# Issue order of two attention looks: where the look for maxima is narrow and the look for weights wide, the wide one goes first

## The chip, the cores and the metric

The kernel runs on one core of one Trainium2 chip. The metric is the time of one execution on the device in microseconds (us), smaller being better; the median of several runs is compared. A profile of one execution shows when each instruction ran on each engine: TensorE (PE; its weight loads are listed apart as PEld), VectorE (DVE), ScalarE (ACT), GpSimd (POOL) and SyncE (SP), which issues most of the DMA transfers.

## What is computed

Two network layers over 16 sequences of 512 tokens with 128 features each. In each layer the input is normalized, two branches are computed from it, and both are added to it.

```
xn = layernorm(x);  x = x + memory_attention(xn) + conv_attention_mixture(xn)     # first layer
xn = layernorm(x);  x = x + causal_conv_attention(xn) + routed_experts(xn)        # second layer
```

The first layer's second branch has a convolution, an attention with 16 heads of 8 features without a mask, and 8 dense experts. Its first branch is a recurrent memory update over chunks of 64 tokens. The second layer's first branch attends twice, causally, with a convolution between:

```
def _causal_attn(q, k, v):
    scores = jnp.einsum('bthd,bshd->bhts', q, k) * scale
    scores = jnp.where(mask, scores, -jnp.inf)
    attn = jax.nn.softmax(scores, axis=-1)
    return jnp.einsum('bhts,bshd->bthd', attn, v)
ctx = _causal_attn(q, k, v);  q2 = conv(ctx);  out = _causal_attn(q2, k, v) @ out_w.T
```

Its second branch routes each token to 8 of 32 small experts.

## The kernel before

Everything is written as stages: Python generators that issue some instructions and then yield. The class `Turns` (line 276) runs them in turns. In a turn each live stage is stepped once, in the order of its priority (0 first). TensorE's instructions stay in the order in which they are issued (line 690: a manual schedule for TensorE); the order on the other engines is chosen by a scheduler in the framework, which also gives out the buffers. Where a priority-1 or later stage issues VectorE instructions, they are held behind the last maxima reduction of the same turn (`newest`, `tc.issue_after`, lines 293 to 295); from priority 2 on GpSimd's also stand behind the last mask (`cleared`, lines 297 and 298).

Attention is done for one sequence, one pass and one half of the heads at a time, in two stages.

- `largest` (priority 0, line 378) finds the maximum of the scores of each query. One **look for maxima** takes one block of 128 queries for one or more heads in two row groups: matmuls into two PSUM banks (`s1`, in the trace `s<-kx,qx`), then on VectorE a reduction into `nm`. Without a mask, and with a mask where one head fills the bank, it is one instruction a bank (line 403 or 395); otherwise an addition of the mask (line 402) and a reduction (line 403).
- `weighted` (priority 1, line 427) makes the softmax weights. One **look for weights** recomputes scores the other way round into two banks (`s2`, in the trace `s<-qx,kx`), ScalarE takes exponentials into `e` (line 475), and in the second layer GpSimd clears the triangle above the diagonal (line 483), or VectorE does late in the kernel, once the routing is counted (line 481). Between the matmuls and the exponentials, eight older weights may be multiplied with the values (`pc`, through `tail` and `values`).

`widths` (line 359) says how wide a look is. Without a mask there are 16 looks of 512 keys for each half of the heads. With the causal mask there are 11: four of 512, four of 384, two of 256 (two heads at once) and one of 128 (four heads at once). So a bank is always filled to 384 or 512 elements, but a 256 or 128 look needs the addition and the reduction. There are 64 such sets in the second layer. A lock (`p1`, `p2`) lets one set of each kind run at a time, so a turn holds at most one look for maxima and one for weights, normally of different sets.

After a set's last look for maxima, `largest` splits the maxima into `mp` (lines 409 and 410), transposes them on TensorE (`tpm`, line 417), copies them to `m` and sends them by DMA through memory into extra rows of `qx`; the looks for weights of that set read `qx`.

Beside the looks a turn holds units of the first layer's experts (`first` and `second` in `ffn`: matmuls `phe` and `pye`, ScalarE `hTe` and `y`), and pieces of all other stages. Scores, expert units and most other products share seven PSUM banks (`work`, line 177); the framework gives a new tile the bank that it expects to be free first, and the tile's first matmul waits until the bank's earlier contents are read. `fill` (line 199) adds idle matmuls where a turn would leave TensorE with little work. How many expert units a turn gets follows from sums over the turn (`load_ns`, `look_ns`), taken after both looks.

The lines around the change are 290 to 300 (a turn's order), 384 to 404 (a look for maxima) and 461 to 492 (a look for weights).

Of the kernel before, what the change touches and what calls it, by code (L numbers as in the profile page):

```python
# [17 lines left out]
P = 128  # L18
# [64 lines left out]
def network(ctx: ExitStack, tc: tile.TileContext, a, out):  # L83
# [55 lines left out]

    pools, done, locks, clock, newest, cleared, held, read, cell = {}, {}, set(), [0], [None], [None], [0], [0], []  # L140

    lent = set()

    def mark(*m):
        done[m] = clock[0]
# [17 lines left out]
    def room():  # L163

        while held[0] >= pools["work"]:
            yield
# [109 lines left out]
    class Turns:  # L276
# [6 lines left out]
        def run(self, until=None):  # L283
            while (self.stages or self.live) and (until is None or not until()):
                self.live += [x[1:] for x in self.stages if x[0] <= self.turn]
                self.stages = [x for x in self.stages if x[0] > self.turn]
                self.live.sort(key=lambda x: x[0])


                newest[0] = cleared[0] = None  # L290
                step = lambda x: next(x[1], StopIteration) is not StopIteration
                left = [x for x in self.live if x[0] == 0 and step(x)]
                with ExitStack() as behind:
                    if newest[0] is not None:
                        behind.enter_context(tc.issue_after(newest[0].ins))
                    left += [x for x in self.live if x[0] == 1 and step(x)]
                    if cleared[0] is not None:
                        behind.enter_context(tc.issue_after(cleared[0].ins))
                    left += [x for x in self.live if x[0] > 1 and step(x)]
                self.live = left  # L300
                self.turn += 1
                fill()
                held[0] -= read[0]
                read[0] = 0
                mean_ns[0] += (other_ns[0] - mean_ns[0]) / 32
                load_ns[0] = look_ns[0] = 0.0
                locks.discard("values")
                clock[0] = self.turn
# [50 lines left out]
    def widths(causal):  # L359

        for i in range(TB):
            n = S if not causal else S - i * P
            per = {S: 1, 3 * P: 1, 2 * P: 2, P: 4}[n]
            for t in range(0, NH, per):
                yield i, n, per, t
# [12 lines left out]
    def largest(slot, causal):  # L378


        q, k, at = slot
        yield from acquire("p1")
        nm = att.tile([P, TB, 2, NH], F32, tag="nm", bufs=2, name="nm")
        for i, n, per, t in widths(causal):
            qt = TB - 1 - i

            look_ns[0] = {S: 2050, 3 * P: 1800, 2 * P: 2450, P: 3000}[n] if causal else 1750
            sv = [work("s1")[:, 0 : per * n].rearrange("p (i n) -> p i n", i=per) for r in range(2)]
            for u in range(per):
                for r in range(2):  # L390
                    rr = slice(64 * r, 64 * r + 64)
                    mm(sv[r][:, u, :], q[rr, t + u, qt * P : (qt + 1) * P], k[rr, t + u, :n])
            for r in range(2):
                if causal and per == 1:
                    newest[0] = nc.vector.tensor_tensor_reduce(  # L395
                        out=sv[r][:, 0, :], in0=sv[r][:, 0, :], in1=row["caus"][:, S - n :], scale=1.0, scalar=-BIG,
                        op0=ALU.add, op1=ALU.max, accum_out=nm[:, qt, r, t : t + 1],
                    )
                    continue
                if causal:  # L400
                    dg = sv[r][:, :, n - P : n]
                    nc.vector.tensor_tensor(dg, dg, bc(row["caus"][:, S - P :], 1, per), ALU.add)  # L402
                newest[0] = nc.vector.tensor_reduce(nm[:, qt, r, t : t + per], sv[r], AX.X, ALU.max)  # L403
            yield
        locks.remove("p1")
        padded = maxima.pop(0)
        maxima.append(padded)
        mp = padded[:, 0 : TB * 16].rearrange("p (t r i x) -> p t r i x", t=TB, r=2, i=2)
        nc.vector.tensor_scalar(mp[:, :, :, 0, :].bitcast(FR), nm, -1.0, None, ALU.mult)
        nc.vector.scalar_tensor_tensor(  # L410
            mp[:, :, :, 1, :].bitcast(FR), nm, -1.0, mp[:, :, :, 0, :], ALU.mult, ALU.subtract
        )
        yield
        yield from room()

        tp = work("tpm")
        nc.tensor.transpose(tp[:, 0:P], padded, ident)
        m = att.tile([TB * 16, P], FR, tag="m", bufs=1, name="m")
        nc.scalar.copy(m, tp[0 : TB * 16, 0:P])
        nc.sync.dma_start(at, m.bitcast(F32))  # L420
        at = at.rearrange("(a r i t) s -> r i t a s", r=2, i=2, t=NH)
        for r in range(2):
            rows = q[64 * r + 32 : 64 * r + 34, :, :].bitcast(F32)
            nc.sync.dma_start(rows.rearrange("i t (a s) -> i t a s", s=P), at[r])
        yield

    def weighted(slot, vp, c, causal, cn, name):


        q, k, _ = slot  # L430
        yield from acquire("p2")
        cnv = cn.rearrange("p t (a c j d) -> p (t a) c j d", c=2, j=2, d=DH)
        old, last = [], []
        got = []

        def values(heads):
            for head in heads:
                kt, n, t, r, e = head
                lent.discard(id(head))
                g = 2 * (t % 2) + r  # L440
                j = t // 2
                mm(
                    got[0][32 * g : 32 * g + 32, S - n :], vp[:, kt, 4 * g + 2 * c + j, :], e,
                    start=(kt == 0 and j == 0), stop=(kt == TB - 1 and j == 1),
                )
            if kt == TB - 1 and t == NH - 1:
                cs = att.tile([P, S], F32, tag="cs", bufs=1, name="cs")
                nc.scalar.copy(cs, got[0])
                locks.remove("ctx")
                last.append(cs)  # L450

        def tail(least):
            if not got and "ctx" not in locks:
                locks.add("ctx")
                got.append(pools["ps"].tile([P, 512], F32, tag="ctx", bufs=1, name="pc"))
            if got and len(old) >= least:
                locks.add("values")
                for _ in range(min(len(old) // 4, 2)):
                    values([old.pop(0) for _ in range(4)])

        for i, (kt, n, per, t) in enumerate(widths(causal)):
            while len(old) >= pools["heads"] and not got and "ctx" in locks:
                yield
            s = [work("s2")[:, 0 : per * n] for r in range(2)]
            sv = [x.rearrange("p (i n) -> p i n", i=per) for x in s]
            for u in range(per):
                for r in range(2):
                    rr = slice(64 * r, 64 * r + 64)
                    mm(sv[r][:, u, :], k[rr, t + u, kt * P : (kt + 1) * P], q[rr, t + u, S - n :])
            tail(pools["heads"])  # L470

            pool = pools["weights"][i % len(pools["weights"])]
            e = pool.tile([P, 2, 512], F32, tag="e", bufs=3, name="e")
            for r in range(2):
                nc.scalar.activation(e[:, r, 0 : per * n], s[r], AF.Exp, scale=SCALE)  # L475
            ev = e[:, :, 0 : per * n].rearrange("p r (i n) -> p r i n", i=per)
            if causal:
                for r in range(2):
                    if ("counted",) in done:
                        dg = ev[:, r, :, 0:P]  # L480
                        nc.vector.scalar_tensor_tensor(dg, bc(row["tri"], 1, per), BIG, dg, ALU.mult, ALU.min)
                        continue
                    cleared[0] = nc.gpsimd.affine_select(  # L483
                        out=ev[:, r, :, 0:P], in_=ev[:, r, :, 0:P], pattern=[[0, per], [1, P]],
                        compare_op=ALU.is_ge, fill=0.0, base=0, channel_multiplier=-1,
                    )
            for u in range(per):
                for r in range(2):
                    old.append((kt, n, t + u, r, ev[:, r, u, :]))
                    if pool is pools["mid"]:  # L490
                        lent.add(id(old[-1]))
            yield
        locks.remove("p2")
        free_slots.append(slot)
        turns.stages.append((turns.turn, 2, ends(summed(old, tail, last, c, cnv), name)))
# [1146 lines left out]
```

## Time and profile before

| what | value |
|---|---|
| runs, us | 3588.07, 3590.16, 3597.58 (median 3590.16) |
| the profiled execution, us | 3586.38 |
| its span from first to last instruction, us | 3584.7 |
| mean granted TensorE clock | 0.969 |
| look for maxima on VectorE, one bank, 512 / 384 keys (line 395), ns | 708 / 579, plus 141 to read the result |
| 256 / 128 keys: addition (line 402), ns | 427 / 694 |
| 256 / 128 keys: reduction (line 403), ns | 680 / 680 |
| exponentials of one bank (line 475), 512 / 384 elements, ns | 600 / 491 |
| TensorE busy from 1850 to 3300 us | 1419.1 of 1450 us, clock 0.99 |
| TensorE busy from 3300 us to the end | 237.6 of 284.7 us, clock 0.86 |

The durations are those from 1850 to 3300 us, in the second layer. The span is the time from the first to the last instruction; the profiled execution's own time has about 2 us more around it. A busy share says how long an engine had an instruction in work. A matmul's listed duration is longer than the distance to the next one, since matmuls are pipelined; distances from start to start tell how fast the stream runs. In a list of waits, "A <- B" means that A's engine stood idle until B's result was there. In the 40 slices of the page each digit is a tenth.

### The profile page before, as it was taken

What the parts mean: (1) busy time and instruction counts of PE and PEld (TensorE: products, weight loads), DVE (VectorE), ACT (ScalarE), POOL (GpSimd) and SP (SyncE); (2) the same over time, 40 slices, a digit from 0 to 9 for tenths busy, and PEclk for the clock granted to TensorE, in tenths of its full rate; (3) what the DMA queues carried; (4) which work ended last, traced back from release to release, by engine and by line L of the source; (5) the groups of instructions that cost most, each with busy time, mean ns of one, the idle gap of its engine ahead of it and who ended that gap; (6) DMA issues with size and microseconds to landing.
All of it is one profiled execution on the core that took longest, in us unless ns stands there. A gap on an engine that the chain in (4) does not pass through costs nothing.

```text
span 3584.7 us, 63937 instructions
## 1 busy us (share of the span) xinstructions
PE 3388.3 (95%) x22085; PEld 1903.2 (53%) x22085; DVE 2319.8 (65%) x6045; ACT 2217.0 (62%) x4919; POOL 1541.4 (43%) x2386
## 2 busy tenths in 40 slices
PE   6999999899999999999999999999999999998887
PEld 3445555454555455555555555555555555553444
DVE  5676666566756565556467676666666666667885
ACT  1566656665666787766656666666666666664444
POOL 5423532433531455433544444434444444433653
PEclk7999999899999999999999999999999999998997
DMA  5222222212222233334344444444344434433343
GB/s 176 70 70 71 74 72 78 67 53 85 76 73 88 89 110 108 110 118 125 106 111 136 126 121 113 121 136 122 95 132 121 134 114 111 132 106 98 92 102 91
DMA packets 289794, 370.37 MB, mean 103 GB/s; under 512 B 45984, under 2 KB 141376, under 8 KB 289088
## 3 DMA queue, kind: packets, MB, share of 16 engines
q1 hardware_dynamic: 282304, 359.46, 34.7%
q0 software_dynamic: 7168, 6.82, 1.2%
q8 instruction: 177, 2.90, 0.3%
q14 instruction: 145, 1.19, 0.1%
HBM read 236.58 MB, written 132.99 MB: 103 GB/s over the span
## 4 chain that ended last, share of the span: by engine, by line
PE 50%; DVE 4%; DMA 2%; ACT 2%; POOL 1%; issue 1%; SPq 1%; POOLq 0%; DVEq 0%; ACTq 0%
PE s L197 13%; PE pye L610 10%; PE phe L197 10%; PE pc L197 8%; PE pq L197 1%; DVE s L395 1%; PE fill L206 1%; PE tpc L251 1%; PE tp L251 1%; DVE nm L403 1%; PE po L197 1%; DVE s L402 1%; ACT e L475 1%; PE pjk L197 1%; PE pv L197 1%
## 5 line engine op out<-in xcount | busy, mean ns | idle before, releaser
L475 ACT ACTIVATE e<-s 128x512 f32<-128x512 f32 (+1 forms) x2432 | 1274.6, 576 | 556.6 <-PE s L197 514.3
L403 DVE TENSOR_REDUCE nm<-s 128x1 f32<-128x512 f32 (+2 forms) x1408 | 906.7, 682 | 512.0 <-PE s L197 510.6
L395 DVE CUSTOM_DVE_ANT_0 s<-s,sb_const 128x512 f32<-128x512 f32 (+1 forms) x1024 | 623.4, 643 | 388.2 <-PE s L197 386.6
L483 POOL TENSOR_SCALAR_AFFINE_SELECT e<-e 128x128 f32<-128x128 f32 (+2 forms) x1270 | 426.7, 344 | 746.6 <-ACT e L475 721.1
L197 PE MATMUL s<-kx,qx 64*128 64x512 f32 (+3 forms) x3072 | 624.4, 431 | 44.4 <-ACT e L475 15.4
L197 PE MATMUL pc<-e,vp 128*32 128x512 f32 (+3 forms) x6144 | 625.8, 506 | 13.4 <-POOL e L483 7.2
L610 PEld LDWEIGHTS pye<-ew,hTe 128*128 128x128 f32 x4096 | 519.8, 193 | 177.9 <-issue 157.6
L197 PEld LDWEIGHTS s<-kx,qx 64*128 64x128 f32 x3072 | 272.8, 187 | 574.4 <-issue 226.6
L610 PE MATMUL pye<-ew,hTe 128*128 128x128 f32 x4096 | 563.0, 281 | 1.5 <-ACT hTe L600 1.4
L197 PE MATMUL s<-qx,kx 64*128 64x512 f32 (+3 forms) x3072 | 536.3, 357 | 26.9 <-DVE nm L403 7.8
L197 PE MATMUL phe<-x1T,ew 128*128 128x512 f32 x1024 | 547.5, 619 | 7.0 <-DMA ew<-in_ew 3.0
L600 ACT ACTIVATE hTe<-phe,sb_cols 128x512 f32<-128x512 f32 x512 | 353.7, 691 | 240.7 <-PE phe L197 238.1
L197 PEld LDWEIGHTS s<-qx,kx 64*128 64x128 f32 x3072 | 305.7, 189 | 78.5 <-ACT e L475 20.4
L618 POOL TENSOR_TENSOR ac<-ac,y 128x512 f32<-128x512 f32 x128 | 163.7, 1279 | 422.6 <-ACT y L617 359.9
L402 DVE TENSOR_TENSOR s<-s,sb_const 128x256 f32<-128x256 f32 (+1 forms) x384 | 181.6, 515 | 190.0 <-PE s L197 157.1
L197 PEld LDWEIGHTS pc<-e,vp 128*32 128x32 f32 x6144 | 150.9, 110 | 238.9 <-issue 174.9
L197 PEld LDWEIGHTS phe<-x1T,ew 128*128 128x128 f32 x1024 | 157.9, 192 | 73.1 <-issue 43.5
L617 ACT ACTIVATE y<-pye,pr 128x128 f32<-128x128 f32 x512 | 146.8, 369 | 31.1 <-PE pye L610 26.9
L395 DVE DVE_READ_ACCUMULATOR2_ANT nm<- 128x1 f32 x1024 | 144.0, 141 | 0.0
L212 POOL TENSOR_SCALAR rs_t<-ss 128x4 f32<-128x4 f32 (+1 forms) x56 | 11.5, 206 | 228.6 <-ACT sq L265 227.3
L1458 POOL DMA_INDIRECT acc<-eo,sidx x32 | 51.6, 1612 | 74.3 <-DVE eo L1452 26.6
L212 POOL TENSOR_SCALAR rs_t<-ln_mv 128x4 f32<-128x4 f32 x64 | 12.7, 198 | 162.5 <-DVE ln_mv L222 159.7
(297 smaller groups left out, 3935.7 us busy)
## 6 DMA issues: line engine op xcount, KB each, us to landing
ew<-in_ew SPq DMA_DIRECT2D x256, 256.0 KB
kx<-rk SPq DMA_DIRECT2D x192, 256.0 KB
qx<-rq SPq DMA_DIRECT2D x128, 256.0 KB
rq<-hi SPq DMA_DIRECT2D x64, 256.0 KB
rq<-lo SPq DMA_DIRECT2D x64, 256.0 KB
rk<-hi SPq DMA_DIRECT2D x64, 256.0 KB
rk<-lo SPq DMA_DIRECT2D x64, 256.0 KB
qx<-r SPq DMA_DIRECT2D x64, 256.0 KB
```

The lines of the kernel that those rows point to most:

```text
L197: nc.tensor.matmul(o, lhsT=lhsT, rhs=rhs, start=start, stop=stop)
L251: nc.tensor.transpose(tp[:, t * P : (t + 1) * P], src(t), ident)
L395: newest[0] = nc.vector.tensor_tensor_reduce(out=sv[r][:, 0, :], in0=sv[r][:, 0, :], in1=row["caus"][:, S - n :], scale=1.0, scalar=-BIG, ...
L402: nc.vector.tensor_tensor(dg, dg, bc(row["caus"][:, S - P :], 1, per), ALU.add)
L403: newest[0] = nc.vector.tensor_reduce(nm[:, qt, r, t : t + per], sv[r], AX.X, ALU.max)
L475: nc.scalar.activation(e[:, r, 0 : per * n], s[r], AF.Exp, scale=SCALE)
L483: cleared[0] = nc.gpsimd.affine_select(out=ev[:, r, :, 0:P], in_=ev[:, r, :, 0:P], pattern=[[0, per], [1, P]], compare_op=ALU.is_ge, fill= ...
L600: nc.scalar.activation(hs[i], ph, AF.Relu, bias=col("fb", i))
L610: nc.tensor.matmul(pye[0][:, t, :], lhsT=h[:, t * P : (t + 1) * P], rhs=w2[e][:, f, :], start=(f == 0 and t == 0), stop=(f == 3), skip_gro ...
L617: nc.scalar.mul(y[:, t, :], pye[0][:, t, :], pr[:, t, e : e + 1])
L618: nc.gpsimd.tensor_tensor(ac, ac, y, ALU.add)
L1458: nc.gpsimd.indirect_dma_start(out=acc, out_offset=bass.IndirectOffsetOnAxis(ap=sidx[:, e : e + 1], axis=0), in_=eo[:, i, :], in_offset=No ...
```

## The change

The last look that each of the two stages has issued now leaves behind how wide its next look will be: `coming[0]` for the maxima, `coming[1]` for the weights, and 0 where the set is at its end. At the start of a turn `narrow` is true when the next look for maxima is of 256 or 128 keys and the next look for weights of 384 or 512. In such a turn the priority-1 stages are stepped before the priority-0 stages, outside the block that holds VectorE's instructions behind the last reduction; in all other turns the order is as before.

```diff
-    lent = set()
+    lent, coming = set(), [0, 0]
...
                 step = lambda x: next(x[1], StopIteration) is not StopIteration
-                left = [x for x in self.live if x[0] == 0 and step(x)]
+                left, narrow = [], 0 < coming[0] < 3 * P <= coming[1]
+                if narrow:
+                    left += [x for x in self.live if x[0] == 1 and step(x)]
+                left += [x for x in self.live if x[0] == 0 and step(x)]
                 with ExitStack() as behind:
                     if newest[0] is not None:
                         behind.enter_context(tc.issue_after(newest[0].ins))
-                    left += [x for x in self.live if x[0] == 1 and step(x)]
+                    if not narrow:
+                        left += [x for x in self.live if x[0] == 1 and step(x)]
                     if cleared[0] is not None:
                         behind.enter_context(tc.issue_after(cleared[0].ins))
...
-        for i, n, per, t in widths(causal):
+        looks = list(widths(causal))
+        for at_look, (i, n, per, t) in enumerate(looks):
...
                 newest[0] = nc.vector.tensor_reduce(nm[:, qt, r, t : t + per], sv[r], AX.X, ALU.max)
+            coming[0] = [*looks, (0, 0)][at_look + 1][1]
             yield
...
-        for i, (kt, n, per, t) in enumerate(widths(causal)):
+        looks = list(widths(causal))
+        for i, (kt, n, per, t) in enumerate(looks):
...
+            coming[1] = [*looks, (0, 0)][i + 1][1]
             yield
```

## The prediction

> **What bounds the kernel now.** I read the page first: busy shares, slices and clock.
>
> ```profile
> span 3584.7 us, 63937 instructions
> PE 3388.3 (95%) x22085; PEld 1903.2 (53%) x22085; DVE 2319.8 (65%) x6045; ACT 2217.0 (62%) x4919; POOL 1541.4 (43%) x2386
> ...
> PE   6999999899999999999999999999999999998887
> ...
> PEclk7999999899999999999999999999999999998997
> ```
>
> TensorE is busy 95% of the span, and the granted clock is 9 tenths or more almost everywhere. The reordered turns lie in the second layer, so next I asked for TensorE's waits between 1850 and 3300 us, most of that stretch.
>
> ```profile
> engine line waited for: us in total, times, longest us
> ...
> PE s L197 <- DMA qx<-top: 5.9, 7, 2.2
> PE phe L197 <- DMA ew<-in_ew: 3.0, 1, 3.0
> ...
> PE tpc L251 <- ACT cs L448: 2.1, 5, 0.5
> ...
> PE tpm L417 <- DVE mp L410: 1.0, 3, 0.4
> PE phe L197 <- ACT e L475: 0.8, 5, 0.2
> PE s L197 <- DVE nm L395: 0.7, 2, 0.3
> ```
>
> The answer's 18 rows add up to 28 us of 1450. That is about the stock from which a change that adds and removes no work could win here. Waits for VectorE's maxima and ScalarE's weights, the two things that are reordered, are about 2 us of it. (A wait counts only from the modelled end of the matmul before, so short ones look smaller than they are; below I take intervals from start to start for that.) In the last stretch, 3300 to 3584.7 us, TensorE is busy 237.6 of 284.7 us, at a clock of 0.86, and VectorE 208.4: that stretch is looser.
>
> Third, the order of time in one such pair of turns: a look for maxima of two heads by 256 keys, then one of four by 128.
>
> ```profile
> start us, us, engine line op out<-in xcount [idle before <-releaser]
> ...
> 2028.66 0.50 PE L197 MATMUL s<-kx,qx 64*128 64x256 f32 x4
> ...
> 2029.00 0.40 PE L197 MATMUL s<-qx,kx 64*128 64x512 f32 x2
> 2029.27 0.43 DVE L402 TENSOR_TENSOR s<-s,sb_const 128x256 f32<-128x256 f32 x1 [0.35 <-PE s L197]
> ...
> 2029.33 0.66 PE L251 MATMUL tpc<-sb_const,cs 128*128 128x128 f32 x4
> 2029.50 1.09 ACT L475 ACTIVATE e<-s 128x512 f32<-128x512 f32 x2 [0.61 <-PE s L197]
> ...
> 2032.09 0.66 PE L197 MATMUL s<-kx,qx 64*128 64x128 f32 x8
> ...
> 2032.59 0.45 PE L197 MATMUL s<-qx,kx 64*128 64x512 f32 x2
> 2032.86 0.70 DVE L402 TENSOR_TENSOR s<-s,sb_const 128x512 f32<-128x512 f32 x1 [0.85 <-PE s L197]
> ```
>
> Matmuls named s<-kx,qx are the look for maxima, s<-qx,kx the look for weights. From start to start the maxima's look holds TensorE for 0.34 us at 256 keys (2028.66 to 2029.00) and 0.50 at 128; the weights' look for 0.33 (2029.00 to 2029.33). VectorE starts 0.61 us after its look, ScalarE 0.50 after its own, and both had been idle.
>
> **The change, part by part.** It adds no instruction on any engine and takes none away: the built programs have the same instructions by kind and tile. On TensorE the order differs in 181 turns: 118 with a 256-key look, 63 with a 128-key look, all but six against a weights' look of 512. By the trace 164 of them lie before 3300 us, the first at 1647. In 180 nothing stands between the two looks. VectorE's order differs in under 3% of its places, ScalarE's in ten instructions, GpSimd's in eight, SyncE's DMAs in nine single issues moved by one to three places; none of the transfers changes its size, and I put these at nothing beside the terms below.
>
> *The stream of matmuls.* I took medians of the time from each pair's start to the next start in the second layer. A look's first pair after other work takes 0.337 us (512 keys, the maxima's; the weights' look hardly ever comes first and is taken as the same), 0.223 (256), 0.164 (128); a pair inside the block 0.119 or 0.117 (256) and 0.110 to 0.112 (128); the last pair, before other work, 0.325 (512), 0.209 (256) and 0.203 (128, seen only before value matmuls). For 256: before 0.223+0.119+0.325 = 0.667, after 0.337+0.117+0.209 = 0.663, no change. For 128: before 0.164+2x0.110+0.112+0.325 = 0.821, after 0.337+3x0.110+0.203 = 0.870, so 0.05 more, times 63: **+3.1 us**. Ends: 0 (leaving after 128 costs no more than staying) and +9 (0.05 in all 181).
>
> *VectorE 0.33 us later.* The maxima are read from PSUM later by the weights' look, 0.33 us. VectorE itself has room: 129.1 us of idle time before the 100 pairs of 256-key additions from 1850 to 3300, 1.3 us a look, and 31.6 us before the 50 of 128 keys, 0.6 a look. What can be late is the next matmul into the same bank. I joined the trace's times with the bank numbers of the built program: from VectorE's last read to the next matmul into the bank is 0.147 us where TensorE had waited. After a 128-key look the usual successor is the next turn's weights' look, 56 times, with 0.51 us in the median: 0.36 of slack, just over 0.33. Over the 328 banks of the reordered looks before 3300, 53 have less than 0.33 us of slack, and the shortfall adds up to 9.3 us; later 9 of 30, 2.3 us. The banks rotate differently afterwards, in the new order nearer for the 128-key look (five to seven tiles on, where it was mostly seven or eight), farther for others. Ends 0 and 11.6; I take half, **+5.8**.
>
> *The chain behind the last look.* The 128-key look ends a set of maxima; mp, the transpose tpm, m and a DMA into qx follow, and the first look for weights waits for that. TensorE waited for mp 7 times in the second layer and for qx<-top 7 times before 3300; 0.33 us on all 14 is 4.6. Ends 0 and 4.6, taken half: **+2.3**.
>
> *ScalarE 0.34 to 0.50 us earlier.* This is the gain. Before 3300, 24 of 328 banks of the weights' looks were taken over by a matmul that had waited for that read, later 8 of 34: at most 32 x 0.36 = 11.5 us. The five waits of tpc for cs, 2.1 us, stand behind the same exponentials, but where I looked ScalarE was at y or hTe and couldn't have begun earlier. Ends 0 and -13.6; I take half, **-6.8**.
>
> *The masks of the last stretch.* From 3384 us on, VectorE clears the weights' upper triangles (L481). The built order now puts these, which wait for the exponentials, ahead of or between the narrow look's additions and reductions. In the turn at 3391.85 us of the trace, additions that started at 3393.12 would start at some 3393.7, with 0.48 us of masks done before them and not after: at most 0.3 late in each of the ten reordered turns from there on, +3; values that are ready earlier may give 2 back. Between these ends I take **+1**.
>
> A rule speaks against any longer wait. The one long stall, 2.99 us for ew, was followed by a clock of 0.72 from 2494 to 2498 us, and four passes of phe took 3.31 us; two take 1.13 in the turn shown. Counting such a loss, some 1.1 us, for each of the seven waits for qx would add up to 8 us. The Trainium skill ("TensorE: Matmul & The Clock Gate", section "Why this matters for your kernels") says that gaps over about 3 us throw the clock back. By it 0.33 us added to waits of at most 2.2 adds nothing; no run here shows where the limit lies. My sum has nothing for it.
>
> Sum: 3.1+5.8+2.3-6.8+1 = **+5.4 us**, on the profiled execution's 3586.4 (span 3584.7, the rest lies around it): 3591.8. The median of the runs shown is 3590.2, so on that scale **3596 us**, 0.2% over. A measurement of this kernel tells about 0.3%, 10.8 us, from no change: the forecast is no change, with its own range 3583 to 3601.
>
> **Rivals.**
> *Late maxima hold TensorE up (slower).* If slack counts for less than I think, since a late look makes the next late too, each turn pays 0.33. The point from which this decides is 10.8/0.33 = 33 turns of 181; the slacks show 62 short banks, some two to a turn. At 50 turns, with 3.1 for the stream: 3590+16.5+3 = 3610. For: five-tile distance after 128 keys. Against: over 0.6 us of idle VectorE before each narrow look.
> *Earlier exponentials pay (faster).* All 13.6 us are won, and delays cost nothing: 3590-13.6 = 3577. For: those waits recur in the same turn of each set. Against: TensorE waits for ScalarE in few places, and the second matmul of a pair often waited for hTe, which isn't earlier.
> *The masks stall VectorE in the last stretch (slower).* If each of those ten turns waits for both exponentials, 0.6 us each by the page, it is +12, with the stream's 3.1 3605; it decides from 0.8 us a turn. For: VectorE already waits 16.0 us there for exponentials before masks. Against: it comes to the masks backlogged in the turns I read.
> That the change doesn't do what it says is ruled out by the 181 turns.
>
> **How the numbers follow.** Forecast 0.50, late maxima 0.24, masks 0.08, earlier exponentials 0.18. So faster by over 0.3% 0.18, within 0.50, slower 0.32. The range reaches from the faster rival to just past late maxima: 3577 to 3613; outside is left about 0.2.
>
> **What would show it.** Right: TensorE's busy time within some 5 us; VectorE's idle time before L402 up by about 0.33 us a look; exponentials of these turns starting 0.5 us after the turn does; the waits of TensorE from 1850 to 3300 still near 28 us. Wrong: waits s<-nm of over 10 us (late maxima); the stretch after 3300 longer by over 6 (masks); waits for e and cs gone and nothing in their place (the gain).

## The result and the profile after

The changed kernel has a median of 3608.56 us (3605.81 to 3611.12, six runs); the kernel before, on the same chip and in turn with it, 3590.18 us. The ratio is 1.0045, 95% interval [1.0032, 1.0058], some 16 us slower. A second set, `after_again` below, gave 1.0026 [1.0013, 1.0039]. So it is slower, by about the 0.3% that the prediction took this kernel's measurement to tell. The time lies inside the whole range, 3577 to 3613, but outside the forecast's own 3583 to 3601: "no change" was the wrong side of the border. The profiled execution took 3607.65 us, with a span of 3605.9 and a mean granted clock of 0.966.

The head of the page of the kernel after, with the slices of TensorE and of its granted clock:

```profile
span 3605.9 us, 63924 instructions
...
PE 3396.2 (94%) x22085; PEld 1920.4 (53%) x22085; DVE 2319.0 (64%) x6045; ACT 2214.3 (61%) x4919; POOL 1541.1 (43%) x2386
...
PE   6999999899999999999999999999999999998887
...
PEclk7999999899999999999999999999999999998988
```

The counts behind the x are those of before, and VectorE, ScalarE and GpSimd are busy as long within 3 us. TensorE's busy time rose by 8 us and the span by 21. Nothing here says where.

TensorE's waits from 1850 to 3300 us, kernel after (engine, line and tile, "<-" what it waited for; us in total, times, longest):

```profile
PE s L197 <- DMA qx<-top: 5.4, 5, 2.2
PE s L197 <- ACT hTe L608: 5.1, 21, 0.8
PE tpm L423 <- DVE mp L416: 2.5, 7, 0.5
...
PE tpc L251 <- ACT cs L454: 1.8, 4, 0.5
PE tpc L251 <- ACT e L482: 1.5, 5, 0.4
...
PE phe L197 <- ACT e L482: 0.7, 2, 0.4
PE s L197 <- DVE nm L400: 0.7, 2, 0.3
PE s L197 <- DVE nm L408: 0.7, 2, 0.4
```

The second line is new: 21 times a look's matmul waits until ScalarE has read an expert unit's bank (`hTe`). Waits for `mp` went from 1.0 to 2.5 us. The waits that the wide looks' earlier exponentials should have taken away (`e`, `cs`) are where they were, and one for `e` was added (`tpc`, 1.5). No row is large, but the sum is: the rows of this answer add up to 29.3 us, those of before to 28, and of the 28 one row has left the window. The first line is of the kernel before, from 1850 to 3300 us, the second of the kernel after, from 3300 us on:

```profile
PE pt L197 <- DVE bd L1346: 6.3, 1, 6.3
...
PE pt L197 <- DVE bd L1354: 5.9, 1, 5.9
```

Without it 22 us of waits became 29. Because a wait counts only from the modelled end of the matmul before, I measured the rest from start to start, below.

The same pair of turns as in the prediction, now from 2032.38 us (timeline of the kernel after; start, duration, what):

```profile
2032.38 0.50 PE L197 MATMUL s<-qx,kx 64*128 64x512 f32 x2
...
2032.71 0.63 PE L197 MATMUL s<-kx,qx 64*128 64x256 f32 x4
...
2032.98 0.74 DVE L338 SCALAR_TENSOR_TENSOR lo<-pjk,sb_cols,hi 128x512 fp32r<-128x512 f32 x1
...
2033.62 0.66 PE L251 MATMUL tpc<-sb_const,cs 128*128 128x128 f32 x4 [0.28 <-ACT e L482]
...
2033.97 0.75 DVE L407 TENSOR_TENSOR s<-s,sb_const 128x256 f32<-128x256 f32 x2
...
2036.05 0.50 PE L197 MATMUL s<-qx,kx 64*128 64x512 f32 x2
...
2036.16 1.14 ACT L625 ACTIVATE y<-pye,pr 128x128 f32<-128x128 f32 x4 [0.20 <-PE pye L618]
2036.39 0.56 PE L197 MATMUL s<-kx,qx 64*128 64x128 f32 x8
...
2037.06 0.70 DVE L407 TENSOR_TENSOR s<-s,sb_const 128x512 f32<-128x512 f32 x1 [1.15 <-PE s L197]
2037.17 0.61 ACT L482 ACTIVATE e<-s 128x512 f32<-128x512 f32 x1
```

And from the 128-key turn of the kernel before, which begins at 2032.09 us:

```profile
2032.20 1.14 ACT L617 ACTIVATE y<-pye,pr 128x128 f32<-128x128 f32 x4 [0.20 <-PE pye L610]
...
2033.21 1.10 ACT L475 ACTIVATE e<-s 128x512 f32<-128x512 f32 x2
```

In the 256-key turn the addition begins 1.59 us after the turn (2032.38 to 2033.97), before 0.61: VectorE had begun other work (`lo`, and before and after it `vp`). The turn takes 3.67 us, before 3.43. In the 128-key turn the exponentials begin 1.12 us after the turn's start, the very delay of before (2032.09 to 2033.21): ScalarE is at `y` in both, so scores that are ready 0.5 us earlier start nothing earlier.

To place the loss I compared each turn's length from 1640 to 3290 us, from the start of its first look to the next turn's, in both traces. The differences fall into two kinds. **Short ones**, up to 0.65 us, recur at the same place in set after set: +2.4 us in all in the second 256-key turn, +3.2 in the 128-key turn, +4.8 in the 512-key turn behind it, together **+9.9 us** with small remainders elsewhere. **Jumps** of one to two us come in single turns, of both signs, and sum up to +8 us. After 3300 us another 3 are lost. The experiments take the two kinds apart.

### The profile page after: what moved, and what is told of

Its sections match the earlier page's. It is cut to its first block, busy times and chain, and to the rows that moved or that the text cites. A ratio compares the mean times of both kernels' runs of the same rounds, so it can differ in the third digit from the quotient of the medians.

```text
span 3605.9 us, 63924 instructions
## 1 busy us (share of the span) xinstructions
PE 3396.2 (94%) x22085; PEld 1920.4 (53%) x22085; DVE 2319.0 (64%) x6045; ACT 2214.3 (61%) x4919; POOL 1541.1 (43%) x2386
## 4 chain that ended last, share of the span: by engine, by line
PE 49%; DVE 5%; DMA 3%; ACT 2%; issue 1%; POOL 1%; SPq 1%; POOLq 0%; DVEq 0%; ACTq 0%
PE s L197 12%; PE pye L618 10%; PE phe L197 10%; PE pc L197 8%; DVE s L400 1%; PE pq L197 1%; DVE nm L408 1%; PE tpc L251 1%; PE tp L251 1%; PE fill L206 1%; ACT e L482 1%; DVE s L407 1%; PE po L197 1%; PE pjk L197 1%; ACT hTe L608 1%
## 5 line engine op out<-in xcount | busy, mean ns | idle before, releaser
L197 PE MATMUL s<-kx,qx 64*128 64x512 f32 (+3 forms) x3072 | 616.5, 421 | 49.2 <-ACT e L482 16.8
L197 PEld LDWEIGHTS s<-kx,qx 64*128 64x128 f32 x3072 | 290.6, 187 | 528.9 <-issue 212.9
L197 PE MATMUL s<-qx,kx 64*128 64x512 f32 (+3 forms) x3072 | 545.3, 367 | 25.8 <-DVE nm L408 7.9
```

Of the source, the lines that this page charges most:

```text
L197: nc.tensor.matmul(o, lhsT=lhsT, rhs=rhs, start=start, stop=stop)
```

## The experiments

All were timed in five rounds against the kernel before on the same chip. "Short waits" is the sum just described, from 1640 to 3290 us, each kernel's trace against the trace of before. Line numbers shift by a few between kernels.

| run | median, us | ratio to before [95%] | short waits, us |
|---|---|---|---|
| `before_again` | 3593.28 | 0.9994 [0.9979, 1.0008] | +0.2 |
| `after_again` | 3606.43 | 1.0026 [1.0013, 1.0039] | +9.2 |
| `x128` | 3598.82 | 1.0012 [1.0000, 1.0024] | +5.8 |
| `x256` | 3602.75 | 1.0016 [1.0006, 1.0027] | +3.4 |
| `late_dve` | 3608.30 | 1.0040 [1.0025, 1.0054] | +9.5 |
| `notlate` | 3602.74 | 1.0018 [1.0006, 1.0030] | +9.2 |
| `lateonly` | 3599.05 | 1.0004 [0.9988, 1.0020] | -1.2 |
| `before_light` | 3575.64 | 0.9941 [0.9920, 0.9962] | -11.2 |
| `after_light` | 3583.54 | 0.9960 [0.9946, 0.9973] | -9.3 (by sum) |
| `reord` | 3600.78 | 1.0018 [1.0005, 1.0030] | +0.8 |

(`after_light` was compared with `before_light`, +1.9; -11.2 and +1.9 make -9.3.)

**Is the measure itself steady?** The kernel before once more:

> The kernel before unchanged, for a second trace of it. Both the late-read theory and its rivals expect 1.000 within 0.001 of itself. Its short waits from 1640 to 3290 us should agree with the first trace within 1.5 us if what I read off as short steady waits is a property of the order; its half-speed time of TensorE may differ by 10 us or more if that is a property of the run. If the short waits differ by 5 us or more, the 9 to 10 us read from the changed kernel's traces can't be told from scatter.

Its short waits agree to 0.2 us, and those of `lateonly` below, which has the order of before up to 3384 us, to 1.2: so 9 to 10 us are no scatter. Its jumps don't agree: +7.1 us against the first trace of the very same kernel, nearly the +8 of the kernel after. So jumps of this size come without the change; the clock below goes with most of them. The kernel after once more:

> The changed kernel once more, beside the others on the same chip and with a second profile. The steady part of the loss (waits for banks in the narrow turns and the turn behind a 128-key look, 10 us between 1640 and 3300 us in the first profile) should be the same to 1 us, since it is fixed by the program. The rest of the first profile's loss (half-speed windows, 8 us there) depends on where the windows of 3.4 us fall and may move. Ratio 1.003 to 1.005.

The short waits come back, 9.2 against 9.9, in the same turns (2.1, 3.8, 4.6). The ratio is smaller than in the first set and than expected, and the two intervals just overlap.

**Which turns?** The swap for one width alone:

```diff
-                left, narrow = [], 0 < coming[0] < 3 * P <= coming[1]
+                left, narrow = [], coming[0] == P and 3 * P <= coming[1]         # x128
+                left, narrow = [], coming[0] == 2 * P and 3 * P <= coming[1]     # x256
```

> The wide look goes first only where the look for maxima has 128 keys (63 of the 181 turns). Late-read theory (the narrow look's two PSUM banks are read 0.3 to 0.4 us later and the next turn's looks wait for a bank): this is the look that VectorE reads longest, and in the changed kernel's trace it and the turn behind it carry most of the steady loss, so over half of the 16 us of the ratio should stay: +8 to +14 us against before. Order-of-matmuls theory (the stream itself is dearer or cheaper): -3 us, since the block of the two looks takes 0.83 instead of 0.88 us in the median. Clock theory (every delay thins the work and the clock is granted at half for more windows of 3.4 us): the half-speed time of the profile, 115 us before and 136 after, lies in proportion to the loss.

> The wide look goes first only where the look for maxima has 256 keys (118 of the 181 turns). Late-read theory: VectorE reads this look 0.7 us faster and the next turn has room, so only some ten turns wait 0.24 us: 0 to +5 us. Order theory: 0. If every reordered turn cost the same, 118 of 181 would cost two thirds of 16, some +10 us.

The 63 turns of 128 keys cost 5.8 us of short waits (1.8 in the turn, 4.0 in the 512-key turn behind it), the 118 of 256 keys 3.4 (2.6 of it in the second 256-key turn). Together 9.2, and the ratios, 0.12% and 0.16%, add up to 0.28%, within what the two sets gave for the whole change: the loss is additive as far as these intervals can tell. By the short waits a 128-key turn costs about three times a 256-key turn. The 8 to 14 us expected of `x128` did not come: its ratio gives 4 us, with an interval from 0 to 9.

**Late maxima, without moving a matmul.** The order of before on TensorE, place by place; VectorE gets one more reduction, whose result is not used, ahead of each narrow look's additions, to start them late:

```diff
+                if causal and r == 0:
+                    late = sm.tile([P, 1], F32, tag="late", name="late")
+                    nc.vector.tensor_reduce(late, sv[0].rearrange("p i n -> p (i n)")[:, 0 : 2 * P], AX.X, ALU.max)
                 if causal:
                     dg = sv[r][:, :, n - P : n]
```

> The order of before, and in each look for maxima of 256 or 128 keys of the second layer VectorE first reads 256 elements of the first bank once more (a reduction into one column that nobody uses, 192 of them, about 0.35 us each), so that both banks are read that much later. Not one matmul moves. Late-read theory: this alone brings a good part of the loss, +5 to +15 us. Order theory, and any theory by which TensorE's order or ScalarE matters: no change, within 4 us of before, since VectorE had 0.6 to 1.3 us idle before these looks.

It reproduces the loss, 1.0040 and 9.5 us of short waits, mostly in the same place (5.5 in the turn behind the 128-key look). (The added reduction, 0.42 us, also makes VectorE's later work late; the two can't be parted here.) One turn of the same set shows how. The timeline of the kernel before: the 128-key look and VectorE's two reductions of it, then the next turn up to its value matmuls `pc`:

```profile
2002.20 0.66 PE L197 MATMUL s<-kx,qx 64*128 64x128 f32 x8
...
2004.17 1.28 DVE L403 TENSOR_REDUCE nm<-s 128x4 f32<-128x512 f32 x2
...
2005.02 0.50 PE L197 MATMUL s<-kx,qx 64*128 64x512 f32 x2
...
2005.37 0.64 PE L197 MATMUL s<-qx,kx 64*128 64x384 f32 x2
...
2005.93 0.64 PE L197 MATMUL pc<-e,vp 128*32 128x512 f32 x4
```

The same in the kernel after:

```profile
2005.45 0.51 PE L197 MATMUL s<-qx,kx 64*128 64x512 f32 x2
...
2005.56 0.27 ACT L1221 COPY lg<-prl 128x128 f32<-128x128 f32 x1 [0.40 <-PE prl L197]
2005.87 0.52 PEld L197 LDWEIGHTS s<-kx,qx 64*128 64x128 f32 x8 [0.24 <-ACT lg L1221]
2005.87 0.66 PE L197 MATMUL s<-kx,qx 64*128 64x128 f32 x8
...
2007.84 1.28 DVE L408 TENSOR_REDUCE nm<-s 128x4 f32<-128x512 f32 x2
...
2008.41 0.50 PE L197 MATMUL s<-kx,qx 64*128 64x512 f32 x2
2008.52 0.69 ACT L608 ACTIVATE hTe<-phe,sb_cols 128x512 f32<-128x512 f32 x1 [1.45 <-PE phe L197]
...
2008.75 0.33 PE L197 MATMUL s<-qx,kx 64*128 64x384 f32 x1
...
2009.26 0.44 PE L197 MATMUL s<-qx,kx 64*128 64x384 f32 x1 [0.18 <-ACT hTe L608]
...
2009.63 0.64 PE L197 MATMUL pc<-e,vp 128*32 128x512 f32 x4
```

And in `late_dve`, with TensorE's order of before:

```profile
2009.78 0.67 PE L197 MATMUL s<-kx,qx 64*128 64x128 f32 x8
...
2012.02 1.27 DVE L406 TENSOR_REDUCE nm<-s 128x4 f32<-128x512 f32 x2
...
2012.61 0.50 PE L197 MATMUL s<-kx,qx 64*128 64x512 f32 x2
...
2012.95 0.34 PE L197 MATMUL s<-qx,kx 64*128 64x384 f32 x1
...
2013.52 0.44 PE L197 MATMUL s<-qx,kx 64*128 64x384 f32 x1 [0.23 <-ACT hTe L603]
...
2013.89 0.64 PE L197 MATMUL pc<-e,vp 128*32 128x512 f32 x4
```

From the second turn's start to `pc`: 0.91 us before (2005.02 to 2005.93), 1.22 after, 1.28 in `late_dve`. The weights' look needs a second bank, and two come free at about that time: the 128-key look's last one, when VectorE's reductions end, and the one that `hTe` reads. Before, the reductions ended at 2005.45, and by the built program's bank numbers the look took that bank 0.15 us later. After, they end at 2009.12, and the framework gave the look the bank that `hTe` reads until 2009.21, 0.05 us before its matmul. VectorE's bank, 0.15 us after its read, would have come no sooner (2009.27). The row "s <- hTe" of the waits is this: the wait names ScalarE, but what is late is VectorE's 128-key look, whose banks are no longer the better choice.

Not every short wait is VectorE's. In the 128-key turn of the same trace the narrow look starts 0.42 us after the wide one (2005.45 to 2005.87), where in the pair of turns above it started after 0.34: its weight load waits for `lg`, with which ScalarE reads `prl` until 2005.83, and by the bank numbers `prl` was in its first bank. This turn is 0.14 us longer than before. How much of the 3.2 us of the 128-key turns is of this kind no run parts.

**Less work on VectorE.** The additions of the mask in the 256- and 128-key looks left out, 384 of them, in the order of before and in the changed one:

```diff
-                if causal:
-                    dg = sv[r][:, :, n - P : n]
-                    nc.vector.tensor_tensor(dg, dg, bc(row["caus"][:, S - P :], 1, per), ALU.add)
                 newest[0] = nc.vector.tensor_reduce(nm[:, qt, r, t : t + per], sv[r], AX.X, ALU.max)
```

> The order of before, without the addition of the mask in the looks for maxima of 256 and 128 keys (384 additions of VectorE, 0.43 or 0.69 us each; the maxima there are then taken over masked keys too). VectorE is done with a narrow look 0.86 or 1.4 us earlier. Late-read theory: the waits of before behind those looks go, 3 to 8 us faster. Order theory: no change, since VectorE is not the bound.

> The changed order without the same 384 additions (the maxima there are taken over masked keys too). Late-read theory: the narrow looks are read earlier than in before in spite of the later issue, so the loss against before_light falls from 16 us to 5 or less; what stays is the look's own first bank, which still waits for ScalarE. Order theory: the loss stays at 14 to 18 us against before_light.

`before_light` at the same place (timeline):

```profile
2006.39 0.66 PE L197 MATMUL s<-kx,qx 64*128 64x128 f32 x8
...
2007.09 1.29 DVE L400 TENSOR_REDUCE nm<-s 128x4 f32<-128x512 f32 x2 [0.93 <-PE s L197]
...
2009.22 0.51 PE L197 MATMUL s<-kx,qx 64*128 64x512 f32 x2
...
2009.56 0.34 PE L197 MATMUL s<-qx,kx 64*128 64x384 f32 x2
...
2009.83 0.64 PE L197 MATMUL pc<-e,vp 128*32 128x512 f32 x4
```

The bank is free at 2008.38, over a microsecond before it is wanted, and the stretch takes 0.61 us: the kernel before already waited 0.30 us there. Over the second layer that is 8.3 us in this turn and 11.2 in all. With the additions gone the swap costs 1.9 us of short waits instead of 9 to 10. So most of the loss needs a VectorE that is already late. (The medians of the two lie 8 us apart, with intervals of some 0.2% each way; read at the same clock of 0.969, as below, 4. What of that is beyond the 1.9 us I can't place.)

`before_light` is also the fastest kernel of the study, 0.59% or 21 us below before, where 3 to 8 were expected. At the same clock of 0.969 it is 13 us faster, so some of the 21 goes with the clock. It computes the same weights in exact arithmetic, since a softmax may be shifted by any number; its maxima in these blocks run over later keys too, so a query whose allowed scores all lie far below a forbidden one would lose its exponentials to underflow. Whether inputs allow that must be decided outside the profile.

**The masks of the last stretch.** The swap only until the routing is counted (171 turns), and only from there on (10 turns):

```diff
-                left, narrow = [], 0 < coming[0] < 3 * P <= coming[1]
+                left, narrow = [], 0 < coming[0] < 3 * P <= coming[1] and ("counted",) not in done   # notlate
+                left, narrow = [], 0 < coming[0] < 3 * P <= coming[1] and ("counted",) in done       # lateonly
```

> The changed order as long as the routing isn't counted, the old order after that (171 of 181 turns keep the new order). Mask theory (in the last stretch VectorE's masks stand in front of the narrow look's reductions and wait for exponentials): the loss falls by 3 us or more, to +13 or less. Late-read theory: the last ten turns are worth their share, under 2 us, so +14 to +17.

> The wide look goes first only after the routing is counted (ten turns from about 3384 us on, where VectorE makes the masks). Mask theory: +5 to +12 us, as the difference between the changed kernel and the one without these ten turns suggests (1.0045 against 1.0018). Late-read theory: 0 to +2 us; then that difference is scatter, mostly of half-speed windows.

`notlate` came out faster than the kernel after, 0.18% against 0.45%, which looked as if the last ten turns cost 9 us. `lateonly` did those ten alone: 1.0004. And `after_again` lies between. Read at the same clock, as below, `notlate` is 12 us above before, beside 11 for `after_again`. The masks cost nothing that can be measured; I had taken scatter for an effect.

**Another order of looks.** If the 128-key look's place is what hurts, it might go ahead of the two 256-key looks:

```diff
-        for i, n, per, t in widths(causal):
+        for i, n, per, t in sorted(widths(causal), key=lambda look: (0, 1, 3, 2)[look[0]]):
```

> The order of the kernel before (maxima first in every turn), but in a causal set of maxima the 128-key look comes before the two 256-key looks instead of after them; nothing is added or left out. Late-read theory (a narrow look's banks are read late because of its addition, and the matmuls of the next turn or two wait): where the four-head look stands among the narrow ones decides who waits; leaving out the additions had given 11 us of such waits, 8 of them in the 512 turn behind the 128-key look, so with a 256-key turn behind it the waits should move and may shrink: 3 to 8 us faster than before, a ratio of 0.998 to 0.999. Rival, position irrelevant (each narrow look costs the same wherever it stands): 1.000 within 0.001. Rival, crowding (three narrow looks on VectorE with the largest backlog first): slower by 3 to 8 us.

The waits moved and didn't shrink: the 512-key turn behind the narrow looks is 5.7 us shorter, and the three narrow turns together 6.4 us longer. The late-read expectation of a gain fell. The ratio, 0.18% slower, is that of the crowding rival, but its waits would have to be short ones, and they sum up to 0.8 us; this key also exchanges two equally wide blocks in the first layer. In its one trace 11.8 us are lost before 1640 us, in that layer, where TensorE spent 133.1 us at half clock, and 112.6 in the first trace of before; whether the exchange does that no run shows.

**The clock.** Most jumps sit where the granted clock is half, eight of the ten in the kernel after. (The other two, +0.9 and +1.0 us in the turns at 2487 and 2836 us of the trace of before, come back in `after_again` with +0.9 and +0.8, and belong to the change.) One place at half clock, in a 128-key turn, by the timeline of before:

```profile
1892.64 0.66 PE L197 MATMUL s<-kx,qx 64*128 64x128 f32 x8
1893.14 0.45 PE L197 MATMUL s<-qx,kx 64*128 64x512 f32 x2
1893.51 1.98 PE L197 MATMUL phe<-x1T,ew 128*128 128x512 f32 x4
```

and of the kernel after:

```profile
1893.59 0.50 PE L197 MATMUL s<-qx,kx 64*128 64x512 f32 x2
1893.93 0.75 PE L197 MATMUL s<-kx,qx 64*128 64x128 f32 x8
1894.77 3.68 PE L197 MATMUL phe<-x1T,ew 128*128 128x512 f32 x4
```

The same four passes of an expert unit take 3.68 us instead of 1.98. By windows, kernel after (window; length, busy time of PE, PEld, DVE, ACT, POOL with counts, then the granted clock, DMA share, GB/s):

```profile
1891.50:1894.90 3.40, 2.84 (x26) 2.32 (x25) 2.79 (x7) 2.67 (x7) 1.74 (x6) 1.00 0.94 260
1894.90:1898.30 3.40, 3.40 (x5) 1.34 (x6) 3.40 (x13) 1.00 (x2) 0.47 (x2) 0.50 0.71 229
```

From 1640 to 3290 us the kernel after spends 41.0 us at half clock, the first trace of before 23.9, and its second trace 41.0 as well. So that much half-clock time comes without the change: 17 us more at half speed cost up to 8.5, which is the size of the jumps. The scatter of 0.6% between runs of one kernel goes with it: among the 27 runs of before beside `after_again`, time and mean clock correlate at -0.88, about 3 us for 0.001 of clock. Straight lines through each kernel's runs, read at the same clock of 0.9665, put `after_again` 11 us above before, `late_dve` 16, `x128` 7, `x256` 5, `notlate` 12, `reord` 7, and `lateonly` and `before_again` 1 below.

## Where the prediction held and where it failed, step by step

The sum's +5.4 us had the right sign and a third of the size. Two terms were mis-sized, the gain on ScalarE and the late reads on VectorE. That the whole range holds 3608.56 is owed to its reaching past the rival of late maxima, not to the sum.

- **Stream of matmuls, +3.1: wrong in sign, small.** The two looks of a 256-key turn take 0.668 us before and 0.666 after in the median, as forecast. For a 128-key turn they take 0.878 before and 0.828 after: 0.05 less, where the sum had 0.05 more, some -3 us. The step added medians of single transitions (0.821) where the whole block was there to be measured.
- **VectorE 0.33 us later, +5.8, "I take half": right in mechanism, too small.** Late work on VectorE alone (`late_dve`) gives a loss of the same size, 9.5 us. But half was too little. The short waits before 3300 are 9.9 us net of all that was won; the upper end had 9.3 for that stretch, of its 11.6. The sum had argued from the bank that follows in the order of before ("0.51 us in the median: 0.36 of slack, just over 0.33") and noted that after the change the next use comes "five to seven tiles on", and then took the middle. The kernel before often had no slack in the turn behind the 128-key look; `before_light` shows 8.3 us of waiting there already. In the turn shown the bank was waited for already: the reductions ended 0.71 us after the next turn's start instead of 0.43, 0.28 later, and the stretch took 0.31 us longer. And an addition was not always 0.33 us late: in the 256-key turn shown it was 1 us late, where VectorE took up other work in between.
- **ScalarE earlier, -6.8: did not come, and is the largest miss.** The term counted the banks that had been waited for and took half of that time as won. The waits for `cs` went from 2.1 to 1.8 us, those of `phe` for `e` from 0.8 to 0.7, and `tpc` waits for `e` 1.5 us where it had not. No place in the sets from 1640 to 3290 became shorter in sum by more than the 0.6 us by which the two traces of before differ. The example shows ScalarE at `y` when the scores come; the prediction had seen the same beside five other waits and not drawn the conclusion for the term.
- **The chain behind the last look, +2.3: right in size.** Waits for `mp` rose from 1.0 to 2.5 us at `tpm` and from 0.6 to 1.5 at `tp`; those for `qx` went from 5.9 to 5.4: together +1.9.
- **Masks, +1: nothing measured** (`lateonly`).
- **The clock: no term, and it needed one in the range.** The sum started from one profiled execution, at a clock of 0.969; the profile after had 0.966. Set against each other raw, the two differ by 21 us, of which about 8 are the second one's clock.

The rival "late maxima hold TensorE up" was the right one, and its 3610 is near the measured 3608.56. It had the place a little wrong: not some fifty turns at 0.33 us alone, but three places of each set, of mostly 0.14 to 0.39 us each when they wait, 46 waits in all. Its sign was "waits s<-nm of over 10 us"; there are 1.4 us of those. The largest new row stands under `hTe` instead, because the framework gave the look another bank in the turn shown. The forecast's sign "waits still near 28 us" seems to hold (29.3) and does not: without the wait for `bd`, which left the window, 22 became 29. Its sign "TensorE's busy time within some 5 us" failed with +8, but the unchanged kernel's second trace has +8 too (3396.3 us), so it told nothing.

The rule that was weighed against the change, that of the Trainium skill ("TensorE: Matmul & The Clock Gate", section "Why this matters for your kernels"), warns of gaps over about 3 us, which throw the clock back. Staying under that was not enough here: in the 3.4 us before the half clock at 1894.9 TensorE was busy for 2.84, and its longest gap was 0.47. From 1640 to 3290 us the kernel after has eight stretches at half clock and no gap longer than 2.4 us. Four of them do follow gaps of 2.0 to 2.4 us, so gaps may matter; at what length, and what else does, no run shows.

## What to carry to other kernels

Before moving work that reads a PSUM bank later, find the next matmul that takes *any* bank at that time, and measure whether it waits already, by start-to-start intervals of the whole block; if it does, expect the delay to count in full, as it did in the turn shown, and don't halve it. Earlier input for an engine is worth nothing while that engine is at other work, as ScalarE was at `y` here. Where two traces differ by less than half a per cent, compare their half-clock time first, and trace the unchanged kernel twice.

## What the runs showed of the hardware

TensorE's granted clock was 1.0 or 0.5 in the stretches that I read, and the stretches at half clock are multiples of 3.41 us (3.41, 6.83, 10.24, 23.89). In the kernel after, from 1640 to 3290 us, they begin after stretches with TensorE busy between 0.98 and 2.98 of 3.41 us; what decides is not shown, and no run tested it. In the turns shown, a matmul that had waited for a bank started 0.15 us after VectorE's last read of it (2005.45 to 2005.60 in the kernel before), and 0.05 us after ScalarE's (2009.21 to 2009.26 in the kernel after).
